# GpSimd's order held for layer 3's first keys, and five early tiles in order around layer 2's first gathered rows

## The chip, the cores and the metric

The kernel runs on one core of one Trainium2 chip. A core has five engines that each work through their own list of instructions in order: TensorE (PE, with weight loads shown apart as PEld), VectorE (DVE), ScalarE (ACT), GpSimd (POOL) and SyncE (SP, which here only issues transfers). They wait for each other through semaphores. The metric is the device time of one execution in microseconds (us). Three runs of the kernel before took 2332.06, 2325.47 and 2327.57 us; the median is 2327.57.

## The reference

Four layers over x of shape (4, 256, 256), each a cross-attention with a context of 1601 rows followed by a feed-forward block. The edit touches layer 2's feed-forward block (a mixture of four experts, one per token) and layer 3's keys (32 heads of 8 elements, normalised head by head).

```python
# layer 2, feed-forward
logits = x @ Wr + br
probs = jax.nn.softmax(logits, axis=-1)
top_w, top_idx = jax.lax.top_k(probs, 1)
g = jnp.einsum('td,edf->tef', x, Wg)
u = jnp.einsum('td,edf->tef', x, Wu)
h = jax.nn.silu(g) * u
y = jnp.einsum('tef,efd->ted', h, Wd)
sel = jnp.take_along_axis(y, top_idx[:, :, None], axis=1)[:, 0]
out = sel * top_w
...
# layer 3, attention
q = x @ Wq.T
k_raw = context @ Wk.T
v_raw = context @ Wv.T
...
q = _rmsnorm(q)
k = _rmsnorm(k)
scores = jnp.einsum('bhnd,bhmd->bhnm', q, k) * scale
attn = jax.nn.softmax(scores, axis=-1)
out = jnp.einsum('bhnm,bhmd->bhnd', attn, v)
```

## The kernel before

The code is written as a program in one order; a scheduler then arranges each engine's instructions by what it expects to be ready, keeping data dependences and adding the waits. `pin` (L165) takes an instruction out of the scheduler's hands: it places it behind whatever the program recorded last on the same engine, whatever that was. `ordered` (L119) pins only while `self.strict` is set, and `mm` (L116), which issues nearly all products, goes through `ordered`.

**Layer 2's experts** are `l2_ffn` (L1016). The 1024 tokens are sorted by expert into 11 blocks of 128 rows (`NS`), the hidden width of 1024 is cut into four chunks (`NC`). After the routing, GpSimd gathers each block's rows from device memory (`f2xr`, L1178, an indirect transfer; three buffers). `brought(n)` (L1190) turns block n with two transposes on PE into `f2tpx`, copies them to `f2xsT`, and loads the block's expert number into a register. `gated(c, n)` (L1197) multiplies by gate and up weights (`f2gu`) and leaves `f2h`, whose last step is a product on VectorE (L1203). `turned` transposes that (`f2tph`, L1209), `down` multiplies by the down weights (`f2y`) and adds into `f2acc`. A loop over 44 steps (L1228) runs gates of step s, transposes of step s - 1 and the down product of step s - 2; through the first ten steps it also brings the next block. Blocks that are finished go to device memory (L1223, SP), eight gathers on GpSimd bring the results back in token order (`f2yt`, L1249), and `l2_add` adds them to x on VectorE at the start of layer 3 (L1261).

**Early tiles.** Products of layer 3 that don't depend on x are made in between. `l3_early(b, ...)` (L1878) is a generator; each of its first 13 steps makes one tile: 8 matrix instructions for 128 context rows' keys and values of batch b (`f2fill` within layer 2, `fill` within layer 3), two copies on ScalarE into `kr` and `va` (L1894), and every second tile a square (L2016) and a sum (L2019). `fill(n)` in `l2_ffn` advances batch 0's generator by n steps. After the 13 tiles the generator loads batch 1's context (L1850, SP), takes the root of the sums and hands over to the spread.

**The spread** of the keys is `l3_spread` (L1948): eight parts, four of the context blocks 0 to 7 and four of 8 to 12. Part by part: `norm` (L1954) scales `kr` on GpSimd (L1957); `halves3` (L1999) splits it into a high half on VectorE (L2007) and a low half on GpSimd (L2008), into the one buffer of `half3`; `turn` transposes on VectorE (L1961) into one of two buffers of `kt3`; `send` issues four transfers on SP to device memory (`kd`, L1969). The norm of the next part is recorded right behind the low half of the present one. The tile `kr3` (L1864) has one buffer, which batch 1's keys take over after batch 0's.

**Layer 3** (`l3`, L2024) begins with `l2_add(0)`, statistics and the queries of batch 0 (L2073), with eleven tiles of batch 1 around them (`FIRST3`, 7, 1 and 3). `keys` (L2226) issues the loads of the first keys (`kf`, L2233), `exact` (L2238) casts them on GpSimd (`kb`, L2242), `asked` (L2245) makes the query's halves and casts (`qb`, L2257). Then the first scores run. From L2367 on every instruction is pinned by a planner that works with costs.

The order around the change is set by: the scheduler within `l2_ffn` once `strict` is cleared at L1185; the pinned routing and loads before that; and, on GpSimd, the scheduler alone, since neither the gathers nor the spread of batch 0 is pinned.

Of the kernel before, what the change touches and what calls it, by code (L numbers as in the profile page):

```python
# [19 lines left out]
ALU = mybir.AluOpType  # L20
# [4 lines left out]
P = 128  # L25
# [30 lines left out]
NH3, HD3 = 32, 8  # L56
# [41 lines left out]
class Kernel:  # L98
# [79 lines left out]
    def fill(self, n):  # L178

        for _ in range(n):  # L180
            next(self.early, None)
# [834 lines left out]
    def l2_ffn(self, other):  # L1016
# [8 lines left out]
        nc, tc = self.nc, self.tc  # L1025
# [4 lines left out]
        with ExitStack() as es:  # L1030
# [9 lines left out]
            def load(c):  # L1040
                wgu = wp.tile([P, E2, 2, 512], F32, name="f2wgu")
                tc.keep_in_program_order(nc.sync.dma_start(wgu, self.i["l2_wgu"][c]))
                wd = wp.tile([P, E2, 2, D], F32, name="f2wd")
                tc.keep_in_program_order(nc.sync.dma_start(wd, self.i["l2_wd"][c]))
                return wgu, wd
# [3 lines left out]
            fill = lambda n: [next(other, None) for _ in range(n)]  # L1049
# [125 lines left out]
            xr = []  # L1175
            for n in range(NS):
                t = two.tile([P, D], F32, name="f2xr", bufs=3)
# [3 lines left out]
                )  # L1181
                xr.append(t)
            chunks.append(load(1))
            fill(3)
            self.strict = False  # L1185
            expert = []
            xsT = one.tile([P, NS, 2, P], F32, name="f2xsT")
            acc = [one.tile([P, D], F32, name=f"f2acc{n}") for n in range(NS)]
# [1 line left out]
            def brought(n):  # L1190
                tp = ps.tile([P, 2, P], F32, name="f2tpx", tag="tp")
                for k in range(2):
                    nc.tensor.transpose(tp[:, k, :], xr[n][:, k * P : (k + 1) * P], self.ident)
                self.evac(xsT[:, n], tp)
                expert.append(nc.tensor.value_load(ei[:, n : n + 1], min_val=0, max_val=E2 - 1))

            def gated(c, n):  # L1197
                gu = ps_g.tile([P, 512], F32, name="f2gu", tag="gu")
                for k in range(2):
                    self.mm(gu, xsT[:, n, k, :], chunks[c][0][:, bass.ds(expert[n], 1), k, :], k == 0, k == 1)  # L1200
                h = two.tile([P, 256], F32, name="f2h", bufs=3)
                nc.scalar.activation(h, gu[:, :256], AF.Silu)
                nc.vector.tensor_tensor(h, h, gu[:, 256:], ALU.mult)  # L1203
                return h

            def turned(h):
                tp = ps.tile([P, 2, P], F32, name="f2tph", tag="tp")
                for m in range(2):
                    nc.tensor.transpose(tp[:, m, :], h[:, m * P : (m + 1) * P], self.ident)  # L1209
                hT = two.tile([P, 2, P], F32, name="f2hT", bufs=3)  # L1210
                nc.scalar.copy(hT, tp)
                return hT

            def down(c, n, hT):
                y = ps_y.tile([P, D], F32, name="f2y")
                for m in range(2):
                    self.mm(y, hT[:, m, :], chunks[c][1][:, bass.ds(expert[n], 1), m, :], m == 0, m == 1)
                if c == 0:
                    nc.vector.tensor_copy(acc[n], y)
                else:  # L1220
                    nc.vector.tensor_tensor(acc[n], acc[n], y, ALU.add)
                if c == NC - 1:
                    nc.sync.dma_start(yd[n * P : (n + 1) * P, :], acc[n])  # L1223

            work = [(c, n) for c in range(NC) for n in range(NS)]
            hs, hTs = {}, {}
            brought(0)
            for s in range(len(work) + 2):  # L1228
                if s < len(work):
                    hs[s] = gated(*work[s])  # L1230
                    if s + 1 < NS:
                        brought(s + 1)
                    elif s < NS + 5:
                        fill(1)
                    elif s >= len(work) - 5:
                        fill(1)
                if 0 <= s - 1 < len(work):
                    hTs[s - 1] = turned(hs.pop(s - 1))
                if s >= 2:
                    down(*work[s - 2], hTs.pop(s - 2))  # L1240
                    c, n = work[s - 2]
                    if n == NS - 1 and c + 2 < NC:
                        chunks.append(load(c + 2))
# [704 lines left out]
    def l3_spread(self, b, st):  # L1948


        nc = self.nc
        kr, ss, x = st["kr"], st["ss"], st["kd"]

        def norm(m0, n, g):  # L1954
            v = kr[:, m0 : m0 + n, g * 64 : g * 64 + P].rearrange("p m (h d) -> p m h d", d=HD3)
            f = ss[:, m0 * NH3 : (m0 + n) * NH3].rearrange("p (m h) -> p m h", h=NH3)[:, :, g * 8 : g * 8 + 16, None]
            nc.gpsimd.tensor_tensor(v, v, f.to_broadcast([P, n, 16, HD3]), ALU.mult)  # L1957

        def turn(t, n):
            tt = self.a3.tile([P, 8, 4 * 32], F32, name="kt3", bufs=2)[:, :, : n * 32]  # L1960
            nc.vector.transpose(  # L1961
                tt.rearrange("p r (m i) -> p r m i", i=32), t.rearrange("p m (r j) -> p r m j", j=32)
            )
            return tt

        def send(tt, m0, n, g):
            for a in range(4):
                c = a * NM * 32 + m0 * 32
                nc.sync.dma_start(  # L1969
                    x[4 * g : 4 * g + 8, :, c : c + n * 32].rearrange("r u k -> u r k"),  # L1970
                    tt[32 * a : 32 * a + 32],
                )

        for m0, m1 in ((0, 8), (8, NM)):
            if b:
                while st["made"] < m1:
                    yield 0.0
                yield 0.9
                v = ss[:, m0 * NH3 : m1 * NH3]
                space = self.a3.tile([P, 4, 2 * P], F32, name="half3").rearrange("p a b -> p (a b)")  # L1980
                yield from self.roots(v, v, 1.0 / HD3, 1e-6, space)
            parts = [(m, min(4, m1 - m), g) for m in range(m0, m1, 4) for g in range(0, 4, 2)]
            norm(*parts[0])
            tt = None
            for at, (m, n, g) in enumerate(parts):
                yield 0.6
                if tt is not None:
                    send(tt, *parts[at - 1])
                t = self.halves3(kr[:, m : m + n, g * 64 : g * 64 + P], 4)
                if at + 1 < len(parts):  # L1990
                    norm(*parts[at + 1])
                yield 1.25
                tt = turn(t, n)
            yield 0.0
            send(tt, *parts[-1])
        st["sent"] = True
        yield 0.0

    def halves3(self, v, most):  # L1999


        nc = self.nc
        n, w = v.shape[1:]
        t = self.a3.tile([P, most, 2 * w], F32, name="half3" if most > 2 else "halfq3")[:, :n]
        tv = t.rearrange("p n (e c d) -> p n e c d", c=2, d=HD3)
        vv = v.rearrange("p n (e d) -> p n e d", d=HD3)
        nc.vector.tensor_scalar(tv[:, :, :, 0, :].bitcast(U32), vv.bitcast(U32), HIGH, None, ALU.bitwise_and)  # L2007
        nc.gpsimd.tensor_tensor(tv[:, :, :, 1, :], vv, tv[:, :, :, 0, :], ALU.subtract)  # L2008
        return t

    def l3_squares(self, ss, v, m0, early, pool=None):
# [669 lines left out]
```

## Time and profile before

| | us |
|---|---|
| runs | 2332.06, 2325.47, 2327.57; median 2327.57 |
| profiled execution | 2325.78 |
| its span, from the first to the last instruction | 2324.1 |
| mean granted TensorE clock | 0.989 of full |
| VectorE, ScalarE, GpSimd busy | 1473.8, 1273.2, 945.0 |
| layer 2's experts, from the first gather to the last down product | 1667.85 to 1818.08 |
| first early tile of batch 1, first score of layer 3 | 1818.58, 1841.23 |
| eight parts of batch 0's spread, first norm to last transpose | 1735.62 to 1791.66 |

The page of the profile lists busy time by engine, then the span in slices, the chain of work that ended last, and groups of instructions by line and shape. Timelines list instructions in order of time: start, length, engine, line, operation, the written and the read tile, and how many were merged; in brackets stands the idle time of the engine before it and, behind the arrow, what ended that idle time. A table of windows gives the busy time of each engine in each stretch, then the granted clock of TensorE (1.00 is full), the share of DMA and GB/s. Matrix products in f32 appear as two records each, and L117 is the line of the helper `mm`, so they are told apart by tile.

### The profile page before, as it was taken

To read this page: it belongs to the slowest core of one execution; us is meant where nothing else is said; L and a number is where in the kernel's file an instruction comes from. 1 tells how busy PE (TensorE), PEld (TensorE's weight loads), DVE (VectorE), ACT (ScalarE), POOL (GpSimd) and SP (SyncE) were. 2 spreads that over 40 slices of the span, in tenths; PEclk is the share of its full clock that TensorE was granted. 3 is DMA by queue.
4 is the path that set the end of the run, shared out by engine and by line. 5 is a ranking of instruction groups with operands and counts; after the bars stand their busy time and mean duration, and the time that the engine had idled before them with its cause. 6 is when DMAs were issued, how large, how long until landed. Compare 5 with 4: busy or idle time off the path is not lost.

```text
span 2324.1 us, 42411 instructions
## 1 busy us (share of the span) xinstructions
PE 2237.6 (96%) x14395; PEld 1376.6 (59%) x14395; DVE 1473.8 (63%) x3571; ACT 1273.2 (55%) x2876; POOL 945.0 (41%) x1719
## 2 busy tenths in 40 slices
PE   8999999889989999999999999999999989999997
PEld 5678978767845555556565656555765634343332
DVE  5553646663568777877788778777334574748343
ACT  2334546433665554445555555554332587888996
POOL 2015645513445554555455545554221254334220
PEclk9999999899999999999999999999999999999999
DMA  7165686632721111111111111100534464434320
GB/s 274 43 207 178 187 150 214 221 113 87 229 99 44 52 53 53 57 52 34 53 48 52 53 52 53 56 3 10 197 127 120 127 160 107 102 95 108 81 68 19
DMA packets 157167, 234.48 MB, mean 101 GB/s; under 512 B 33993, under 2 KB 122825, under 8 KB 155754
## 3 DMA queue, kind: packets, MB, share of 16 engines
q1 hardware_dynamic: 140902, 190.86, 26.1%
q0 software_dynamic: 11280, 31.60, 6.2%
q10 hardware_dynamic: 4772, 9.31, 1.3%
q8 instruction: 118, 1.93, 0.3%
q14 instruction: 95, 0.78, 0.1%
HBM read 169.94 MB, written 61.74 MB: 100 GB/s over the span
## 4 chain that ended last, share of the span: by engine, by line
PE 62%; DVE 4%; POOL 2%; DMA 1%; ACT 1%; issue 1%; SPq 0%; POOLq 0%; ACTq 0%; DVEq 0%
PE o L117 18%; PE s L117 17%; PE o L77 7%; PE b L77 4%; PE f2gu L117 3%; PE s L77 3%; PE acc L117 2%; PE tpq L117 2%; PE f2y L117 1%; PE tpkv L117 1%; PE fill L117 1%; PE f2fill L117 1%; DVE half L77 1%; PE tpqT L1580 1%; DMA kf<-kd 0%
## 5 line engine op out<-in xcount | busy, mean ns | idle before, releaser
L1626 ACT ACTIVATE p<-s,nmsm 128x448 f32<-128x448 f32 (+2 forms) x512 | 324.9, 640 | 391.6 <-DVE nmsm L1621 318.5
L117 PE MATMUL o<-pT,va 128*128 128x256 f32 (+2 forms) x1920 | 432.5, 378 | 0.3
L117 PE MATMUL s<-kT,qT 128*32 128x448 f32 (+2 forms) x4096 | 423.5, 549 | 4.6 <-ACT p L1626 4.6
L77 ACT ACTIVATE e<-s 128x1024 f32<-128x1024 f32 (+1 forms) x416 | 393.0, 1041 | 51.9 <-PE s L77 50.6
L117 PEld LDWEIGHTS o<-pT,va 128*128 128x128 f32 (+1 forms) x1920 | 345.4, 190 | 124.6 <-issue 72.8
L1664 POOL TENSOR_SCALAR p<-p,rm 128x416 f32<-128x416 f32 x508 | 317.0, 645 | 6.3
L1621 DVE TENSOR_REDUCE nmsm<-s 128x1 f32<-128x448 f32 (+4 forms) x384 | 292.9, 783 | 3.8
L1670 DVE STREAM_TRANSPOSE pT<-p 128x448 f32<-128x448 f32 (+4 forms) x384 | 277.9, 778 | 9.3 <-POOL p L1664 9.3
L117 PEld LDWEIGHTS s<-kT,qT 128*32 128x32 f32 x4096 | 121.9, 109 | 250.1 <-issue 213.2
L77 PE MATMUL o<-e,va 128*32 128x512 f32 (+1 forms) x1664 | 247.8, 609 | 5.2 <-DVE os L77 5.1
L1654 POOL TENSOR_TENSOR rm<-em,tot 32x8 f32<-32x8 f32 x256 | 49.9, 195 | 334.6 <-DVE tot L1651 279.8
L1618 DVE TENSOR_TENSOR s<-s,mask 128x64 f32<-128x64 f32 (+4 forms) x384 | 92.0, 259 | 124.1 <-PE s L117 74.3
L77 PEld LDWEIGHTS s<-qb,kb 32*128 32x128 f32 (+1 forms) x1664 | 65.0, 180 | 175.4 <-issue 131.9
L545 POOL DMA_INDIRECT f0xr<-f0xd,f0src x95 | 91.5, 963 | 58.2 <-PE f0tph L604 44.9
L1353 PE MATMUL fill<-wkc_early,ctxT 128*128 128x256 f32 (+1 forms) x444 | 105.4, 388 | 9.6 <-ACT va_early L1361 5.3
L77 PE MATMUL s<-qb,kb 32*128 32x256 f32 (+1 forms) x1664 | 110.6, 330 | 4.1 <-POOL kb L77 1.4
L1626 ACT ACTIVATION_READ_ACCUMULATOR p<-s,nmsm 128x1 f32 x512 | 101.3, 198 | 0.0
L77 POOL CAST kb<-kf 128x384 fp32r<-128x384 f32 (+1 forms) x126 | 64.5, 540 | 87.9 <-DMA kf<-kd 28.9
L1353 PEld LDWEIGHTS fill<-wkc_early,ctxT 128*128 128x128 f32 (+1 forms) x444 | 83.4, 191 | 25.6 <-ACT va_early L1361 7.6
L117 PE MATMUL f2gu<-f2wgu,f2xsT 128*128 x176 | 84.4, 604 | 0.8 <-issue 0.5
L77 PEld LDWEIGHTS o<-e,va 128*32 128x32 f32 (+1 forms) x1664 | 41.4, 108 | 68.6 <-issue 35.1
L117 PE MATMUL f0gu<-f0w,f0xsT 128*128 x380 | 77.8, 326 | 1.9 <-DMA vd<-va_early 1.2
(570 smaller groups left out, 3655.1 us busy)
## 6 DMA issues: line engine op xcount, KB each, us to landing
kf<-kd SPq DMA_DIRECT2D x384, 48.0 KB
vd<-va_early SPq DMA_DIRECT2D x96, 128.0 KB
kd<-kT_early SPq DMA_DIRECT2D x48, 256.0 KB
kT<-kd SPq DMA_DIRECT2D x16, 768.0 KB
va<-vd SPq DMA_DIRECT2D x16, 768.0 KB
kd<-kt SPq DMA_DIRECT2D x96, 128.0 KB
f0yd<-f0ys SPq DMA_DIRECT2D x95, 128.0 KB
ctxT<-in_ctxT SPq DMA_DIRECT2D x5, 1664.0 KB
```

Of the source, the lines that this page charges most:

```text
L77: ins = f(*a, **kw)
L117: self.ordered(self.nc.tensor.matmul(out, lhsT, rhs, start=start, stop=stop, **kw))
L545: nc.gpsimd.indirect_dma_start(out=t, out_offset=None, in_=xd[:, :], in_offset=bass.IndirectOffsetOnAxis(ap=src[:, n : n + 1], axis=0),)
L1353: ins = nc.tensor.matmul(tp[:rows, t, :], ctxT[u // NKV2][:, k, c0 : c0 + rows], w[u % NKV2][:, k, :], start=k == 0, stop=k == 1,)
L1580: tc.keep_in_program_order(nc.tensor.transpose(tp[:, h, :], qo[q][:, h, :], self.ident))
L1618: nc.vector.tensor_tensor(sv, sv, mask[:, e0:e1, : nt - CT, :].rearrange("p n t i -> p n (t i)"), ALU.add)
L1621: nc.vector.tensor_reduce(ms[:, 0, e0:e1], s[:, n0:n1, : nt * 32], AX.X, ALU.max, negate=True)
L1626: nc.scalar.activation(p[:, n, : nt * 32], s[:, n, : nt * 32], AF.Exp, bias=ms[:, 0, e : e + 1], accum_out=ms[:, 1, e : e + 1],)
L1654: nc.gpsimd.tensor_tensor(r[32 * a : 32 * a + 32], e[:, a], tot, ALU.mult)
L1664: nc.gpsimd.tensor_scalar(p[:, n, : nt * 32], p[:, n, : nt * 32], r[:, e : e + 1], 1.0, ALU.mult, ALU.mult)
L1670: self.pin(nc.vector.transpose(pT[:, 2 * c + n0 : 2 * c + n1, :nt, :].rearrange("p n t i -> p n (t i)"), p[:, n0:n1, : nt * 32],))
```

## The change

Four edits.

- The early tiles ahead of the first gathered rows become four instead of three, and `strict` stays set.
- The transposes in `brought` go through `ordered`, so that they are pinned while `strict` is set; one more tile is made between the first block's transposes and its gates. `strict` is cleared at step 1 of the loop, so what is pinned of the loop is step 0: the gates of block 0 and the transposes of block 1.
- The generator's steps are the same; since `fill` has been called two more times ahead of the loop, tiles 11 to 13 fall on steps 10 to 12, the spread's first norm on step 13 and the first part on steps 14 and 15.
- For batch 0 alone (`not b`), the norm and the low half of the spread are pinned on GpSimd: each behind what the program recorded last on that engine. The parts up to the fourth are recorded within the loop. The remaining four are recorded where the program drains the generator (L1254 of the kernel before), behind the eight gathers of L1249.

```diff
             chunks.append(load(1))
-            fill(3)
-            self.strict = False
+            fill(4)
...
                 for k in range(2):
-                    nc.tensor.transpose(tp[:, k, :], xr[n][:, k * P : (k + 1) * P], self.ident)
+                    self.ordered(nc.tensor.transpose(tp[:, k, :], xr[n][:, k * P : (k + 1) * P], self.ident))
...
             brought(0)
+            fill(1)
             for s in range(len(work) + 2):
+                if s == 1:
+                    self.strict = False
                 if s < len(work):
...
-            nc.gpsimd.tensor_tensor(v, v, f.to_broadcast([P, n, 16, HD3]), ALU.mult)
+            ins = nc.gpsimd.tensor_tensor(v, v, f.to_broadcast([P, n, 16, HD3]), ALU.mult)
+            if not b:
+                self.pin(ins)
...
-                t = self.halves3(kr[:, m : m + n, g * 64 : g * 64 + P], 4)
+                t = self.halves3(kr[:, m : m + n, g * 64 : g * 64 + P], 4, not b)
...
-    def halves3(self, v, most):
+    def halves3(self, v, most, held=False):
...
-        nc.gpsimd.tensor_tensor(tv[:, :, :, 1, :], vv, tv[:, :, :, 0, :], ALU.subtract)
+        ins = nc.gpsimd.tensor_tensor(tv[:, :, :, 1, :], vv, tv[:, :, :, 0, :], ALU.subtract)
+        if held:
+            self.pin(ins)
```

## The prediction

> **What bounds the kernel.** I read the page first: busy times, slices, chain. Then the granted clock by stretches, the timelines of TensorE, VectorE and GpSimd around the edited code, and the chain of waits through layer 2's last products. Last I compared the order in which the two built programs issue on each engine, and looked up which instruction each wait names.
>
> ```profile
> span 2324.1 us, 42411 instructions
> PE 2237.6 (96%) x14395; PEld 1376.6 (59%) x14395; DVE 1473.8 (63%) x3571; ACT 1273.2 (55%) x2876; POOL 945.0 (41%) x1719
> ```
>
> TensorE is busy for 96% of the span, so an edit that leaves its work alone can only remove or add idle time and half-clock time of PE. The edit touches layer 2's experts (1666 to 1819 us) and, through what it pushes back, the start of layer 3 (1819 to 1841 us).
>
> ```profile
> 1672.20:1674.60 2.40, 0.03 (x1) 0.06 (x2) 0.69 (x1) 1.17 (x3) 0.00 (x0) 1.00 1.08 427
> 1674.60:1677.40 2.80, 0.79 (x4) 0.34 (x4) 0.42 (x1) 0.37 (x1) 1.13 (x2) 1.00 0.45 167
> 1677.40:1680.90 3.50, 3.44 (x4) 1.51 (x5) 0.01 (x1) 0.00 (x0) 0.76 (x1) 0.51 0.17 40
> 1728.00:1743.90 15.90, 12.85 (x49) 7.71 (x47) 8.03 (x12) 7.10 (x15) 8.28 (x9) 1.00 0.56 214
> 1818.60:1841.20 22.60, 21.63 (x102) 18.81 (x102) 10.53 (x26) 12.60 (x33) 9.44 (x13) 1.00 0.40 111
> ```
>
> Each row is a stretch, its length, busy time of PE, PEld, DVE, ACT and POOL, then the granted PE clock, DMA share and GB/s. After 5.2 us with little to do PE runs 3.5 us at a clock of 0.51. From 1728 to 1743.9 it idles 3.05 us. From 1818.6 to 1841.2 it is all but full, so anything late there is paid by PE.
>
> ```profile
> 1674.57 0.41 PE L1193 MATMUL f2tpx<-ident,f2xr 128*128 128x128 f32 x2 [2.41 <-DMA f2xr<-f2xd,f2src]
> 1676.54 0.41 PE L1193 MATMUL f2tpx<-ident,f2xr 128*128 128x128 f32 x2 [1.55 <-DMA f2xr<-f2xd,f2src]
> 1677.45 5.37 PE L117 MATMUL f2gu<-f2wgu,f2xsT 128*128 x8 [0.51 <-issue]
> 1743.88 0.44 PE L1209 MATMUL f2tph<-ident,f2h 128*128 128x128 f32 x2 [3.05 <-DVE f2h L1203]
> ```
>
> The brackets give the idle time before an instruction and what ended it: 2.41 + 1.55 + 0.51 = 4.47 us at the first gathered rows, and 3.05 us on one VectorE product.
>
> ```profile
> 1736.73 1.28 DVE L2007 TENSOR_SCALAR half<-kr 128x512 uint32<-128x512 uint32 x1
> 1740.97 1.26 POOL L2008 TENSOR_TENSOR half<-kr,half 128x512 f32<-128x512 f32 x1
> 1742.27 1.25 DVE L1961 STREAM_TRANSPOSE kt<-half 128x1024 f32<-128x1024 f32 x1 [4.25 <-POOL half L2008]
> 1744.08 0.41 DVE L2007 TENSOR_SCALAR half<-kr 128x512 uint32<-128x512 uint32 x1
> ```
>
> Here is the cause of the 3.05: POOL does five norms in a row (5.39 us from 1735.62) before its first low half, the transpose waits 4.25 us for that, and the product that PE wants stands behind the transpose on VectorE.
>
> ```profile
> 1821.15 0.98 POOL L1249 DMA_INDIRECT f2yt<-f2yd,f2slot  x1 [34.22 <-DMA kf<-kd]
> 1829.94 0.95 POOL L1249 DMA_INDIRECT f2yt<-f2yd,f2slot  x1 [0.30 <-issue]
> 1818.58 12.35 PE L117 MATMUL fill<-wkv,ctx 128*128 128x256 f32 x56 [0.51 <-DVE f2acc L1221]
> 1841.23 1.04 PE L77 MATMUL s<-qb,kb 32*128 32x256 f32 x10 [1.00 <-POOL qb L2257]
> ```
>
> GpSimd's eight gathers run from 1821.15 to 1829.94 + 0.95 = 1830.89. PE meanwhile makes tiles of batch 1's keys, seven in 12.35 us (1.76 each), then queries and four more, and reaches the first score at 1841.23.
>
> **Part 1, two early tiles moved forward, in order.** No tile is added: 13 in both programs. A ninth stands ahead of the first transposes, a tenth between these and the first gates; two fewer follow at full PE load. In before's times: 1672.16 + 1.81 (5.43 for three) = 1673.97, wait to 1674.57 for the rows, 0.41 of transposes, tile to 1676.79. The gates then find their operand ready (its ScalarE copy ended at 1675.39), and the second rows' transposes no longer stand ahead of them. Of 4.47 us idle 0.6 stays: gain 3.87. With PE that full the clock should not halve: 3.5 x (1 - 0.51) = 1.7. Together 5.6; I take **-5.5**. Bounds: -3.9 if the clock falls anyway, and -5.6. Pinning the transposes costs nothing in itself: their rows land later than the tile ahead of them ends.
>
> **Part 2, GpSimd's order held, first four parts.** The spread of the first keys has eight parts, each a norm, a split on VectorE, a low half on POOL, a transpose, four DMAs. In the new order norm and low half alternate, so the first transpose waits for one norm and one half, not five norms. The idle of 3.05 plus 0.64 at the next part is 3.7 at most. But each transpose still waits for its own low half (1.26), and one such wait cost PE 0.64; four cost 2.6. Gain between 1.1 and 3.7, nearest the upper since VectorE has slack between products: **-2.5**. SP sees two sends and one transfer of batch 1's context change places with a weight load; the weights landed tens of us before use, so I count nothing, and part 1's 5.5 us if that cover were gone.
>
> **Part 3, the other four parts.** Held order means: behind everything that the program recorded on GpSimd before. The low halves and norms of parts five to eight are recorded after the eight gathers. In before they ran at 1740 to 1787; in the new order all eight of their instructions follow the last gather. What they wait for and who waits:
> - The chain from 1830.89: norm 1.07, split 0.41, half 1.27; transpose 1.24; split and half 1.68; transpose 1.24; and for the two 128x128 parts 0.67, 0.44, 0.67. Sum 8.7, with some ten handoffs of 0.04 to 0.14 about 9.5. End: **1840.4**. Sends cover themselves: four issues of 0.45 and some 2.2 to land (the last result rows: issued 1818.6, gathered from 1821.15) free the transpose's buffer at about 1839.2, when it is wanted.
> - The keys' tile has one buffer. ScalarE's first copy of batch 1's keys (1820.75 before) waits for the very last low half, so it starts 19.7 us late.
> - PE has three PSUM tiles for these products: it fills them by 1818.58 + 5.29 = 1823.87 and stops. The fourth needs both copies of the first (0.65) and starts at 1841.15, not 1823.87: **+17.3**. All that follows on PE, 1823.87 to 1841.23, is as long as before, since tiles and query keep their order but for halves of a tile.
> - After 17 idle us the clock is halved, by the row at 1677.4: **+1.7**.
> - The two casts of the first keys now stand behind the query's; the first score waits for one more pair: **+0.9** (0.95 for two).
> - VectorE: adding layer 2's result to x waits behind the transposes, with it statistics and query. ScalarE reaches the root after five tiles' copies, 1840.4 + 8.4, rows at 1850; PE wants them after tiles four to seven and half the eighth, 1841.15 + 1.7 + 7.9 = 1850.8. Covered by 0.8; if not, it adds what it lacks.
> - SP: sixteen sends now stand ahead of the sixteen loads of first keys (7.39 to issue). These end near 1854, before the casts at 1860.
>
> Sum of part 3: 17.3 + 1.7 + 0.9 = **+19.9**, bounds 17.3 (clock and casts hidden) and 24 (the sends land 4 us later).
>
> A rule of the Trainium skill, SBUF — State Buffer, section "SBUF: two separate sides", bears on this price. The row first: the split at 1736.73 took 1.28 while POOL ran norms, 0.41 at 1744.08. The page says that VectorE in a two-port mode and GpSimd lock the shared port pair for a whole instruction, the other blocked. Were all four late splits caught so, that would be an estimated 4 x 0.87 = 3.5 more, net +15.4 and not +11.9. The new order keeps them apart, as each split lies between its own norm and the half that waits for it.
>
> **Sum.** -5.5 - 2.5 + 19.9 = +11.9. The profiled execution took 2325.78 us (span 2324.1 and 1.7 around it) and gives 2337.7; the median of the runs shown is 1.8 higher, 2327.57, and gives 2339.5. I say **2339**. Own range: gains 3.9 + 1.1 to 5.6 + 3.7, tail 17.3 to 24: +8.0 to +19.0, on the median 2335.6 to 2346.6.
>
> **Rivals.** (A) *Faster: the late parts get done before they matter.* If the buffer came free by about 1829 (tail under 8.0), parts 1 and 2 would win: with no tail -8.0, 2319.6. For it: before, the same wait cost nothing, as the last half was done at 1787. Against: the first late norm can't start before the last gather's 1830.89. Chance 0.05.
> (B) *The tail is shorter and cancels.* Gains at 9.3, and a tail at 14 because gathers finish some us earlier and the query no longer shares PE with tiles: +4.7, 2332.3. Against: gathers keep a pitch of 1.25, and the eleven tiles remain. Chance 0.08.
> (C) *The sends hold the late transposes.* Each sixth and later transpose needs an earlier part's four sends landed. One such wait occurs in before (0.6 us). If landing takes 6 us rather than 2.2, two transposes slip by some 4: tail 24 to 28 with the query's cover gone, +16 to +20, near 2346. Chance 0.20.
> (D) *The change doesn't do what it says*, the clock still halving and the product still late: +14 to +16; inside the forecast's range and its chance.
>
> **Chances.** Forecast 0.67, A 0.05, B 0.08, C 0.20. Slower by over 0.3% (7 us, about what a measurement of this kernel tells from no change): 0.67 + 0.20 = 0.87; B is most of "same". The range 2332 to 2348 takes in the forecast, most of C and B's edge.
>
> **What would show it.** Right: idle of PE before the first transposes at 0.6, clock 1.00 through the first gates; no idle of 3 us on that product; GpSimd's last four norms after the gathers; ScalarE's first key copy of batch 1 ended by "POOL half" some 20 us after layer 2's last product; PE's fourth tile after about 17 idle us at half clock. Wrong: that copy waiting for PE alone, or gathers preceded by all sixteen key instructions; then A.

## The result and the profile after

The changed kernel is slower: 2343.94 us in the median of six runs (2340.02 to 2350.26) against 2327.06 of six runs of the kernel before, a ratio of 1.0068 with a 95% interval of 1.0053 to 1.0083, or +12 to +19 us. The profiled execution took 2340.02 us, its span is 2338.3 us, the mean granted clock 0.984. The forecast was 2339 with a range of 2332 to 2348.

Work ahead of the edited code differs from one profile to the next, by up to 20 us over all runs shown here, so absolute times of two profiles can't be compared. The table cuts each span at three events that every kernel has: the start of the routing's last products (`f2st`, PE), the first tile of batch 1's keys (behind layer 2's last accumulation), and layer 3's first score. Its stages are differences of printed times, the last one exact to 0.05 us. The last column is the ratio of times to the kernel before, measured beside it.

| kernel | f2st to tile | tile to score | score to end | ratio (95%) |
|---|---|---|---|---|
| before | 153.66 | 22.65 | 482.87 | 1 |
| after | 145.40 | 43.97 | 484.76 | 1.0068 (1.0053 to 1.0083) |

The gain in the experts is 8.3 us, the loss behind them (the tail) 21.3, and 1.9 us came later. The same views of the changed kernel, in the order of the prediction's parts. The page's first lines:

```profile
span 2338.3 us, 42409 instructions
PE 2241.4 (96%) x14395; PEld 1379.5 (59%) x14395; DVE 1473.6 (63%) x3571; ACT 1272.5 (54%) x2876; POOL 946.4 (40%) x1719
```

TensorE's busy time is 3.8 us more with the same 14395 instructions, which fits the lower mean clock (0.984 against 0.989); the other 10.4 us of longer span are idle time. TensorE's timeline at the first gathered rows:

```profile
1673.83 0.41 PE L1192 MATMUL f2tpx<-ident,f2xr 128*128 128x128 f32 x2 [0.69 <-ACT va L1896]
1675.75 1.97 PE L117 MATMUL f2fill<-wkv,ctx 128*128 128x256 f32 x8 [1.52 <-DMA f2xr<-f2xd,f2src]
1677.55 1.88 PE L117 MATMUL f2gu<-f2wgu,f2xsT 128*128 x4
1679.27 0.60 PE L1192 MATMUL f2tpx<-ident,f2xr 128*128 128x128 f32 x4
1680.17 1.12 PE L117 MATMUL f2gu<-f2wgu,f2xsT 128*128 x2 [0.30 <-DVE f2xsT L112]
```

The window over this stretch, with the granted clock behind the five engines' busy times:

```profile
1671.80:1677.50 5.70, 3.49 (x17) 2.63 (x16) 0.69 (x1) 1.84 (x6) 0.95 (x1) 1.00 0.84 325
```

The first gates take 1.88 us for four products where 5.37 stood for eight, and nothing runs at half clock. But between the transposes and the new tile lies an idle of 1.52 us that the prediction did not have. GpSimd's timeline, from the first norm of the spread to its last low half:

```profile
1725.11 1.07 POOL L1959 TENSOR_TENSOR kr<-kr,ss 128x512 f32<-128x512 f32 x1 [27.51 <-DVE ss L126]
1726.73 1.27 POOL L2012 TENSOR_TENSOR half<-kr,half 128x512 f32<-128x512 f32 x1 [0.54 <-DVE half L2011]
1727.96 1.07 POOL L1959 TENSOR_TENSOR kr<-kr,ss 128x512 f32<-128x512 f32 x1
...
1812.12 0.98 POOL L1251 DMA_INDIRECT f2yt<-f2yd,f2slot  x1 [69.36 <-DMA f2yd<-f2acc]
...
1820.89 0.94 POOL L1251 DMA_INDIRECT f2yt<-f2yd,f2slot  x1 [0.30 <-issue]
1821.85 1.09 POOL L1959 TENSOR_TENSOR kr<-kr,ss 128x512 f32<-128x512 f32 x1
...
1830.93 0.45 POOL L2012 TENSOR_TENSOR half<-kr,half 128x128 f32<-128x128 f32 x1 [0.53 <-DVE half L2011]
```

Norm and low half alternate. GpSimd then stands idle for 69.36 us, up to the first gather, although all keys are there; the other norms and halves begin behind the last gather and end at 1831.38, 9.5 us after it. ScalarE's timeline at that moment:

```profile
1831.42 0.37 ACT L1896 COPY kr<-fill 128x256 f32<-128x256 f32 x1 [23.63 <-POOL half L2012]
```

The first copy of batch 1's keys starts 0.04 us after GpSimd's last low half, and that half is named as what ended 23.63 idle us. TensorE's timeline behind the last accumulation:

```profile
1809.57 5.45 PE L117 MATMUL fill<-wkv,ctx 128*128 128x256 f32 x24 [0.51 <-DVE f2acc L1220]
1832.12 10.73 PE L117 MATMUL fill<-wkv,ctx 128*128 128x256 f32 x36 [17.11 <-ACT va L1896]
1842.68 0.60 PE L2091 MATMUL b<-ident,xn 128*128 128x128 f32 x4
...
1853.54 0.48 PE L77 MATMUL s<-qb,kb 32*128 32x256 f32 x4 [2.18 <-POOL kb L2248]
```

Three tiles (24 products), then 17.11 us of nothing, then the fourth. Where the kernel before made its 24 products in 5.34 us, 36 would take 8.0; here they take 10.73. The first score waits 2.18 us and for the keys' cast, where it waited 1.00 and for the query's. The windows over the same stretch, with the clock in the same place:

```profile
1814.60:1832.10 17.50, 0.41 (x2) 0.01 (x1) 4.24 (x7) 0.68 (x3) 11.94 (x14) 0.57 0.42 107
1832.10:1835.00 2.90, 2.88 (x7) 2.35 (x8) 1.83 (x5) 1.58 (x5) 0.00 (x0) 0.50 0.48 80
1835.00:1838.00 3.00, 3.00 (x10) 2.41 (x9) 1.56 (x6) 1.17 (x3) 0.00 (x0) 0.57 0.40 72
```

The clock stays near one half for some 5.5 us after the tiles have begun again.

### The profile page after: what moved, and what is told of

It reads as the page before. It is cut to its first block, busy times and chain, and to the rows that moved or that the text cites. A ratio compares the mean times of both kernels' runs of the same rounds, so it can differ in the third digit from the quotient of the medians.

```text
span 2338.3 us, 42409 instructions
## 1 busy us (share of the span) xinstructions
PE 2241.4 (96%) x14395; PEld 1379.5 (59%) x14395; DVE 1473.6 (63%) x3571; ACT 1272.5 (54%) x2876; POOL 946.4 (40%) x1719
## 4 chain that ended last, share of the span: by engine, by line
PE 62%; DVE 5%; POOL 2%; issue 1%; ACT 1%; DMA 1%; SPq 0%; POOLq 0%; DVEq 0%; ACTq 0%
PE o L117 18%; PE s L117 17%; PE o L77 7%; PE b L77 4%; PE f2gu L117 3%; PE s L77 3%; PE acc L117 2%; PE tpq L117 2%; PE f2y L117 2%; PE tpkv L117 1%; DVE half L77 1%; PE fill L117 1%; PE tpqT L1582 1%; PE f2fill L117 1%; PE f2tph L1208 0%
## 5 line engine op out<-in xcount | busy, mean ns | idle before, releaser
L655 POOL DMA_INDIRECT f0yt<-f0yd,f0slot x64 | 65.3, 1020 | 35.3 <-DMA kd<-kT_early 15.7
```

What stands on the lines that cost most here:

```text
L655: self.pin(nc.gpsimd.indirect_dma_start(out=yt, out_offset=None, in_=yd[:, :], in_offset=bass.IndirectOffsetOnAxis(ap=slot[:, t, r : r + 1 ...
```

## The experiments

Twelve runs in three groups. Each group had its own runs of the kernel before, with medians of 2330.42, 2340.32 and 2341.16 us; so only ratios, and the stages of the table, are compared across groups.

| kernel | f2st to tile | tile to score | score to end | ratio (95%) |
|---|---|---|---|---|
| first group | | | | |
| first four parts held | 147.81 | 22.64 | 482.82 | 0.9974 (0.9960 to 0.9988) |
| tiles alone | 149.23 | 22.64 | 484.98 | 0.9995 (0.9984 to 1.0007) |
| all eight ahead | 145.48 | 22.65 | 484.31 | 0.9965 (0.9953 to 0.9977) |
| pins alone | 150.24 | 45.92 | 484.91 | 1.0105 (1.0089 to 1.0122) |
| second group | | | | |
| late parts in their own tile | 147.02 | 45.47 | 485.61 | 1.0067 (1.0046 to 1.0087) |
| late parts left out | 147.18 | 25.08 | 484.98 | 0.9982 (0.9962 to 1.0003) |
| late halves twice | 145.00 | 46.76 | 484.58 | 1.0078 (1.0048 to 1.0109) |
| all ahead, tile before the register load | 143.82 | 25.05 | 484.69 | 0.9963 (0.9944 to 0.9981) |
| third group | | | | |
| before, again | 154.22 | 24.93 | 484.41 | 0.9988 (0.9973 to 1.0002) |
| tiles alone, again | 149.09 | 24.93 | 486.66 | 0.9976 (0.9963 to 0.9989) |
| all eight ahead, again | 145.20 | 24.87 | 482.83 | 0.9962 (0.9947 to 0.9978) |
| all ahead, tile before the load, again | 144.24 | 24.89 | 483.86 | 0.9960 (0.9946 to 0.9973) |

**Only the first four parts held.** The pins stay for context blocks 0 to 7 and go for 8 to 12.

```diff
-            if not b:
+            if not b and m0 < 8:
                 self.pin(ins)
...
-                t = self.halves3(kr[:, m : m + n, g * 64 : g * 64 + P], 4, not b)
+                t = self.halves3(kr[:, m : m + n, g * 64 : g * 64 + P], 4, not b and m < 8)
```

> The first four parts of the first keys keep GpSimd's order, parts five to eight are left free, so that their norms and low halves come ahead of the eight gathers again. Theory (the late four parts behind the gathers make the tail): the 44.4 us from the last accumulation to layer 3's first score go back to about 23.1, the 17 us wait of the fourth product of batch 1's keys is gone, the clock stays 1.00 there; but the five norms of parts five to eight now come ahead of the first low half (some 4.0 us of waiting at the first transpose), so part 2's gain is mostly lost. Time: 2327.1 - 3.5 to - 7 = 2320 to 2324. Rival 1 (the early tiles or the held first four cost, not the late four): stays above 2335. Rival 2 (the tail has another cause, such as the sends' queue): the first score still more than 35 us after the last accumulation.

The loss behind the experts is gone to the last 0.01 us: 22.64 against 22.65. The kernel is faster than the one before, by 3 to 9 us. GpSimd's timeline of this run:

```profile
1731.70 4.06 POOL L1959 TENSOR_TENSOR kr<-kr,ss 128x512 f32<-128x512 f32 x5 [27.51 <-DVE ss L126]
1735.72 1.26 POOL L2012 TENSOR_TENSOR half<-kr,half 128x512 f32<-128x512 f32 x1
```

As expected, the scheduler put the free norms of parts five to eight ahead of the first low half, 4.06 us in a row, and TensorE's wait on VectorE's product is back in part (1.72 and 0.25 us). Both rivals fall: neither the tiles nor the sends make the tail.

**The tiles alone.** The pins on GpSimd are taken out, the moved tiles and ordered transposes stay.

```diff
-            if not b:
-                self.pin(ins)
...
-                t = self.halves3(kr[:, m : m + n, g * 64 : g * 64 + P], 4, not b)
+                t = self.halves3(kr[:, m : m + n, g * 64 : g * 64 + P], 4)
```

> The two tiles moved forward and the transposes in order, no GpSimd order held. Theory: part 1 alone is worth what the idle at the first gathered rows and the half clock gave, 5.5 us by the prediction, some 3.5 to 4 by the profile of the changed kernel, where 2.5 us of idle remain: 2322 to 2324. The 3 us wait on VectorE's product stays. No tail: 23 us from last accumulation to first score. Rival (the tiles only move time, since two tiles fewer at the end leave PE waiting for the query there): 2326 to 2328.

The stage from the routing to the tile is 4.4 us shorter, and there is no tail. The whole is -3.7 to +1.6 us, less of a gain than was expected; the profile shows 2.1 us more after the first score. That was tried again below. TensorE's timeline of this run shows the same 1.5 us between transposes and tile:

```profile
1676.97 0.41 PE L1192 MATMUL f2tpx<-ident,f2xr 128*128 128x128 f32 x2 [0.86 <-DMA f2xr<-f2xd,f2src]
1678.94 1.97 PE L117 MATMUL f2fill<-wkv,ctx 128*128 128x256 f32 x8 [1.56 <-DMA f2xr<-f2xd,f2src]
...
1735.53 0.44 PE L1208 MATMUL f2tph<-ident,f2h 128*128 128x128 f32 x2 [2.02 <-DVE f2h L1202]
1739.73 0.44 PE L1208 MATMUL f2tph<-ident,f2h 128*128 128x128 f32 x2 [1.18 <-DVE f2h L1202]
```

The last two lines are the waits on VectorE's product, 3.20 us together; in the changed kernel, with the pins, TensorE has none.

**All eight parts ahead of the gathers.** The generator is advanced in every step of the loop and not in the first five after the gathered rows, so that all norms and low halves are recorded, in alternation, before the gathers.

```diff
-                    elif s < NS + 5:
+                    elif s < NS + 22:
```

> All eight parts recorded, held in alternation, ahead of the gathers (the drain runs until the last products and not only in the first five steps). Theory: both gains stay (9 us at the last accumulation) and the tail is 23 us: 2327.1 - 8 to - 9 = 2318 to 2319.5. Rival 1: VectorE's four more splits and transposes among the experts make PE wait for its products, about 1 us for each: 2322 to 2323. Rival 2: the late parts' work in the experts fills VectorE or GpSimd so that accumulations or gathers come late: at 2327 or above.

Both gains stay (145.48, as the changed kernel's 145.40) and the tail is 22.65. The time is 5 to 11 us below the kernel before. The four more splits and transposes among the experts cost TensorE nothing: its timeline has no wait on VectorE's product.

**The pins alone.** The tiles and the transposes are as in the kernel before.

```diff
-            fill(4)
+            fill(3)
+            self.strict = False
...
-                    self.ordered(nc.tensor.transpose(tp[:, k, :], xr[n][:, k * P : (k + 1) * P], self.ident))
+                    nc.tensor.transpose(tp[:, k, :], xr[n][:, k * P : (k + 1) * P], self.ident)
...
-            fill(1)
             for s in range(len(work) + 2):
-                if s == 1:
-                    self.strict = False
```

> GpSimd's order held in all eight parts, without the moved tiles. Theory: in the built order five low halves and four norms follow the gathers (one part more than in the changed kernel), so the tail is 21 us plus at most one half's chain (some 1.3 to 2.5 us), less some 2.5 to 3.7 from the experts, and none of part 1's gain: 2327.1 + 21 to 24 - 2.5 to 3.7 = 2345 to 2348. Rival (the tiles taken from the end, not the order, leave PE without work there): the tail is near 23 us, the time 2322 to 2327.

The tail grows by 23.3 us, the experts gain 3.4, and the ratio says +21 to +28 us: the lower edge of that is the upper edge of what the theory gave, so the loss was put some us too low. One more low half stands behind the gathers (the loop now makes the two tiles first, and the spread begins later), and TensorE waits 18.86 us and not 17.11:

```profile
1822.77 5.45 PE L117 MATMUL fill<-wkv,ctx 128*128 128x256 f32 x24 [0.51 <-DVE f2acc L1221]
1847.07 11.01 PE L117 MATMUL fill<-wkv,ctx 128*128 128x256 f32 x36 [18.86 <-ACT va L1894]
```

With this run and the tiles alone the change splits into its parts: tiles -4.4, pins -3.4 in the experts, together -7.8 where the change has -8.3.

**The late parts in their own tile.** Norms and splits of parts five to eight work in their own half tile and no longer touch batch 0's key tile, which is free after the fourth low half. Each late norm multiplies the scales by themselves, so the kernel leaves out the values of these keys. The number and order of GpSimd's instructions stay.

```diff
+        def apart(m0, n, g):
+            t = self.a3.tile([P, 4, 2 * P], F32, name="half3")[:, :n]
+            tv = t.rearrange("p n (e c d) -> p n e c d", c=2, d=HD3)
+            lo = tv[:, :, :, 1, :]
...
+            self.pin(nc.gpsimd.tensor_tensor(lo, f, f, ALU.mult))
+            return t, tv
...
+                if not b and m >= 8:
+                    t, tv = made.pop(0)
+                    hi, lo = tv[:, :, :, 0, :], tv[:, :, :, 1, :]
+                    nc.vector.tensor_scalar(hi.bitcast(U32), lo.bitcast(U32), HIGH, None, ALU.bitwise_and)
+                    self.pin(nc.gpsimd.tensor_tensor(lo, lo, hi, ALU.subtract))
```

> The changed kernel, but the late four parts' norms and splits work inside their own half tiles (from squared scales) and no longer read batch 0's key tile, so the keys' single buffer is free after the fourth low half; the same number of GpSimd, VectorE and DMA operations stands behind the gathers in the same order. This leaves out the rotation of part of the first keys. Theory as predicted (the single buffer alone makes the 17.3 us): no wait of the fourth product, the last accumulation to the first score takes 23 to 26 us, the time is near 2320. Rival (the buffer and VectorE's queue limit side by side: the addition to x still stands behind the late transposes, which end some 22 us after the last accumulation, and in the kernel before 15.4 us lie from that addition to the first score): PE runs its products on time, then waits for the query; the first score comes 36 to 39 us after the last accumulation, the time is 2335 to 2339.

Neither theory hit the number, but the rival's mechanism is what the timeline shows. TensorE:

```profile
1822.62 19.26 PE L117 MATMUL fill<-wkv,ctx 128*128 128x256 f32 x88 [0.51 <-DVE f2acc L1220]
1854.93 1.22 PE L2110 MATMUL b<-ident,xn 128*128 128x128 f32 x4 [13.05 <-DVE xn L2085]
1856.94 3.78 PE L117 MATMUL b<-wq,xT 128*128 128x256 f32 x8 [0.78 <-DVE xT L2112]
1865.22 0.69 PE L2278 MATMUL b<-ident,halfq 128*128 128x128 f32 x2 [4.50 <-POOL halfq L2031]
```

The buffer's wait is gone: eleven tiles run without a break. So it was the one buffer that held the fourth tile. But then TensorE waits 13.05 us for the normalised x, and has no tiles left to put into the query's own waits. VectorE's timeline says why:

```profile
1851.22 0.69 DVE L2044 TENSOR_REDUCE ss<-sq 128x64 f32<-128x512 f32 x1 [0.70 <-ACT sq L2041]
1851.82 0.43 DVE L1978 STREAM_TRANSPOSE kt<-half 128x256 f32<-128x256 f32 x1
1852.18 0.84 DVE L1263 SCALAR_TENSOR_TENSOR x<-f2yt,f2gate,x 128x256 f32<-128x256 f32 x2
```

The addition of layer 2's result to x stands behind the last late transpose in VectorE's order, and here also behind five sums of batch 1's squares, which ran one by one with ScalarE's squares from 1845.64 on. It came 29.6 us after the first tile; in the changed kernel 24.6.

The run is no clean removal. Each late norm but the first now also waits for the transpose before it, so the late chain took 11.3 us (1834.91 to 1846.25) and not 9.5; with the five sums between them, the last transpose started 5.6 us after its low half; and after 13.05 idle us the query's products ran at half clock (1.22 and 3.78 us in the lines above, 0.60 and 1.89 in the changed kernel). The query's transposes start 32.3 us after the first tile here, 33.1 there.

The changed kernel shows a second limit close by: its normalised x was ready at 1841.79 (1841.06 + 0.73 on VectorE), 0.9 us before TensorE took it. Yet x was late there in part through the buffer itself: a sum that waited 2.32 us for ScalarE's square of batch 1's keys stood ahead of the last late transpose on VectorE, and ScalarE came to the root behind those keys' copies. So it is shown that the buffer held the fourth tile, and that freeing it in this way gave nothing; how much the buffer alone would give back is not shown.

**The late parts left out.** Parts five to eight have no norm, split, low half or transpose; their sixteen sends carry the fourth part's transpose.

```diff
+            if not b and m0:
+                for part in parts:
+                    yield 0.6
+                    send(last[:, :, : 32 * part[1]], *part)
+                continue
...
+            last = tt
```

> The changed kernel without the late four parts' norms, splits, low halves and transposes; their sixteen sends stay and carry the fourth part's transpose again. This leaves out part of the first keys' rotation. Theory (work behind the gathers makes the tail): 22.7 us from last accumulation to first score, the casts of the first keys ahead of the query's again; 2327.1 - 8 to - 9.5 = 2318 to 2319. Rival (the sends on SP's queue ahead of the loads of the first keys hold the first score): the score still comes more than 26 us after the last accumulation.

The first score comes 25.08 us after the tile, and so it does in the kernel before in the third group (24.93) and with all parts ahead in this group (25.05); of the 21.3 us nothing is left, and the sends do not make them. The time is -9 to +1 us against before, less of a gain than expected. In this profile the clock did fall at the first gathered rows (below), but the profiled run was the fastest of the ten, so that does not account for the median; what does stays open.

**The late halves twice.** Each of the late four low halves is computed a second time.

```diff
+        if held == 2:
+            self.pin(nc.gpsimd.tensor_tensor(tv[:, :, :, 1, :], vv, tv[:, :, :, 0, :], ALU.subtract))
...
-                t = self.halves3(kr[:, m : m + n, g * 64 : g * 64 + P], 4, not b)
+                t = self.halves3(kr[:, m : m + n, g * 64 : g * 64 + P], 4, (not b) * (1 + m // 8))
```

> The changed kernel, each of the late four low halves computed twice on GpSimd: 2 x 1.26 + 2 x 0.45 = 3.4 us more behind the gathers. Theory (the serial chain behind the gathers sets ScalarE's first copy, and that PE): PE's wait grows from 17.1 by 3.4 us to 20.5, the time from 2343.9 by 3.4 to 5 (another half-clock stretch) to 2347 to 2349. Rival (VectorE's queue or the sends set the end, and GpSimd has room beside them): less than 1.5 us more.

TensorE's wait grows by 3.8 us for 3.4 us of work:

```profile
1851.51 9.18 PE L117 MATMUL fill<-wkv,ctx 128*128 128x256 f32 x34 [20.90 <-ACT va L1896]
```

GpSimd's chain behind the gathers took 13.3 us and not 9.5, and TensorE paid that one for one. The stage to the first score grew by 2.8, as fewer products fell into the half clock. The ratio of 1.0078 fits both +3.4 and nothing (1.0048 to 1.0109 against 1.0068); the wait decides, not the time.

**All ahead, and the tile before the register load.** In the changed kernel TensorE's list between the first transposes and the new tile holds the load of the expert's number into a register, with what goes along with it. Here the loads are kept behind what the program recorded before them, and the tile comes first.

```diff
-                expert.append(nc.tensor.value_load(ei[:, n : n + 1], min_val=0, max_val=E2 - 1))
+                if n == 0:
+                    fill(1)
+                last = [i for i in nc.cur_bb.bb.instructions if i.engine == tile_ins[0].ins.engine][-1]
+                with self.tc.issue_after(last):
+                    expert.append(nc.tensor.value_load(ei[:, n : n + 1], min_val=0, max_val=E2 - 1))
...
-            fill(1)
...
-                    elif s < NS + 5:
+                    elif s < NS + 22:
```

> All eight parts ahead of the gathers, and at the first gathered rows the tile stands ahead of the load of the expert's index into TensorE's register, which in the changed kernel stood between the first transposes and the tile. Theory (the 1.5 us idle between the first transposes and the tile is that register load): the tile follows the transposes at once, the idle at the first rows falls from 2.6 to about 1.1 us, and the time is 1.5 us below the kernel with all eight parts ahead: 2327.1 - 9.5 = 2317 to 2318.5. Rival (the tile waits for the next gathered rows or another transfer): the idle of 1.5 us stays, ahead of the tile or behind it, and the time is that of the kernel with all eight parts ahead.

TensorE's timeline at the first gathered rows:

```profile
1689.93 0.41 PE L1193 MATMUL f2tpx<-ident,f2xr 128*128 128x128 f32 x2 [0.43 <-DMA f2xr<-f2xd,f2src]
1690.24 1.99 PE L117 MATMUL f2fill<-wkv,ctx 128*128 128x256 f32 x8
1692.26 1.96 PE L117 MATMUL f2gu<-f2wgu,f2xsT 128*128 x4
```

The 1.5 us are gone, and no idle of that size takes their place; so they were the register load with the queue instructions around it (listed under the hardware below), and not the transfer that the bracket named. The stage is 1.7 us shorter than with all eight ahead. The whole, 0.9963, did not show it beside a tail of 25.05, and so this kernel was run again.

**Third group: the kernel before once more, and three kernels beside it.** No edits.

> The kernel before, unchanged, profiled a second time beside the three that follow. Two things are open: after layer 3's first score eight of ten profiles so far take 484.3 to 485.6 us, the kernel before and the one with the first four parts held 482.9; and in the second group of runs two kernels whose order behind the last accumulation is that of the kernel before took 25.1 us there and not 22.65. Theory (both are chance or the chip's, not the edit's): the kernel before shows 484 to 485 us after the first score, or 25 us behind the last accumulation, in this profile too. Rival (the edits bring them): 482.9 and 22.65 again; ratio 1.000.

> The moved tiles alone a second time. Theory (the stage's gain of 4.4 us is real and what the first measurement lost of it, -1.1 with -3.7 to +1.6, were half-clock stretches in layer 3 that come and go): -2 to -5 us against before. Rival (the tiles moved forward are paid for in layer 3 each time): within 1.5 us of before.

> All eight parts ahead of the gathers, a second time, as the yardstick for the next: -6 to -9 us against before, ratio near 0.9965.

> All eight parts ahead and the tile ahead of the register load, beside the kernel that lacks only the second. Theory (the load's 1.5 us are gone for good and the 2.4 us lost behind the last accumulation came with the chip): 1.5 us below the kernel with all eight parts ahead, ratio against before 0.9955 to 0.996. Rival (moving the load costs as much later): the same time as that kernel, with 25 us behind the last accumulation again while that one has 22.65.

The kernel before itself shows 24.93 us behind the experts here and 484.41 after the first score: neither difference belongs to an edit. After the first score the same kernel took 484.31 and 482.83 in its two profiles, another 484.98 and 486.66, the kernel before 482.87 and 484.41. The tiles alone gain 3 to 9 us this time (0.9976) after -4 to +2; the rival that layer 3 takes their gain back each time falls. All eight ahead repeats itself (0.9965, 0.9962). With the tile ahead of the load the ratio is 0.9963 and 0.9960: the stage is 1.0 to 1.7 us shorter both times, but the times alone can't tell the two kernels apart.

So a version beats both kernels: the change with all eight parts recorded ahead of the gathers, 0.35 to 0.4% below the kernel before and over 1% below the changed one; the register load moved is worth 1.0 to 1.7 us more in its stage, which the times alone don't show.

## Why the prediction was right, point by point

- **Part 1, -5.5.** The half clock went in the changed kernel, as said; of the nine profiles with the same instructions there, two show it again (below), so that part was luck in any one run. Of the idle 4.47 us 2.5 stayed and not 0.6. The step that failed is the tile following the transposes at once: a register load and its checks, 1.5 us, lay between them in TensorE's order, and with only 0.41 us of transposes queued nothing covered them. Moved behind the tile, they were hidden. The kernel before has the same instructions at the same place, ahead of its second transposes; the 1.55 us that the line shown in the prediction puts down to the second rows' transfer were these (checks from 1674.6, the load's last instruction at 1676.4, the transposes at 1676.54). Measured, with the tiles alone: -4.4 and, beside the second profile of the kernel before, -5.1 (154.22 to 149.09).
- **Part 2, -2.5 with 1.1 to 3.7.** Too small a gain; the measured ones lie at the upper bound. The pins took -3.4 alone, and -3.8 on top of the tiles. The price of 2.6 us for four waits of a transpose on its own low half was not paid: VectorE waits 1.05 and 1.06 us at the first two and not at the others, and TensorE has no wait on its product. VectorE's timeline of the changed kernel:

```profile
1726.22 0.43 DVE L2011 TENSOR_SCALAR half<-kr 128x512 uint32<-128x512 uint32 x1 [0.26 <-POOL kr L1959]
1728.03 1.25 DVE L1965 STREAM_TRANSPOSE kt<-half 128x1024 f32<-128x1024 f32 x1 [1.05 <-POOL half L2012]
1729.20 0.38 DVE L1202 TENSOR_TENSOR f2h<-f2h,f2gu 128x256 f32<-128x256 f32 x1
```

- **Part 3, +19.9.** Measured +21.3. The chain of the late four parts took 9.5 us from the last gather's end (1821.83) to the last low half's (1831.38), as worked out. The wait was 17.11 us (17.3 said). The half clock was the term that was mis-sized: 10.73 - 8.0 = 2.7 us where 1.7 stood, as it lasted some 5.5 us after the tiles began again and not 3.5. That is not set by the length of the idle time: with the late halves twice, after 20.90 idle us, it lasted 3.2 us by the clock records. The casts cost 2.18 - 1.00 = 1.2 (0.9 said).
- **The buffer as the cause.** Shown: with the buffer free the fourth tile doesn't wait. The query path "covered by 0.8" was right as a number (0.9) and matters more than it looked: it is a second limit close behind, and in the run with the late parts in their own tile it took over.
- **The rule on the shared port.** The Trainium skill, SBUF — State Buffer, "SBUF: two separate sides", would have added an estimated 3.5 us had all four late splits been caught. That priced all four by the 128x512 split, though two are 128x128. The late splits took 0.43, 0.43, 0.23 and 0.23 us, none the 1.28 of the kernel before: none met GpSimd at work, as the prediction held. The rule was not put to the test by these.
- **The rivals.** A fell with ScalarE's 23.63 us wait on the last low half, B with a tail of 21.3. C fell: late transposes waited 1.38, 1.37 and 0.58 us, each for a low half and none for a send, and without the late work the sends cost nothing. D fell.
- **The sum.** Said +11.9, measured +13.1 up to the first score. The profile has 1.9 us more after it, which the third group showed to come and go. The forecast is 4.9 us below the median, inside its range. That the two gains sum to 8.3 where 8.0 was said is luck: part 1 fell short by 1.1 us and part 2 exceeded by 1.3.

## What to carry to other kernels

To hold an engine's order means to hold it behind everything the program recorded before: look at where the generator of that work is drained, not at where its inputs are ready. Here one number in a loop (how many steps drain it) decides between +0.7% and -0.35%. Where one late engine delays two consumers by nearly the same time, freeing one can show nothing, as with the own tile here; read what would be late next before spending a buffer on it. An idle gap whose bracket names a transfer can be a register load and semaphore checks in the engine's own list; the view of that line of the kernel shows them.

## What the runs showed of the hardware

- **The first register load held TensorE's list for 1.5 us, most of it semaphore checks.** The gap was 1.50 to 1.56 us in the nine profiles with only 0.41 us of transposes ahead of it and a tile behind, and nothing is to be seen in the two with the tile ahead. The instructions of the load's line, in the kernel before and in the changed one (`q` marks an instruction that the list works through without counting as the engine's work; times are the first and last start):

```profile
L1195 PEldq EVENT_SEMAPHORE  x10: 51/51/51, 1674.6 to 1675.5; - x10
...
L1194 PEldq EVENT_SEMAPHORE  x10: 51/51/51, 1673.8 to 1674.8; - x10
L1194 PEldq TENSOR_LOAD <-f2ei x11: 297/301/305, 1674.9 to 1703.2; - x11
L1194 PEldq SEQ_ASSERT  x11: 18/18/18, 1675.6 to 1703.8; - x11
```

  Ten semaphore checks start 0.11 us apart, from 1673.8 on; each lasts 0.05 us, so none waits for anything. The first load starts behind them at 1674.9, its last instruction at 1675.6, the tile at 1675.75. So about 1.1 of the 1.5 us are checks. They stand ahead of the first of the eleven loads alone; the other ten loads have none, and gates of some 1.9 us ahead, and show no such gap. Whether the checks could be left out was not tried.
- **After much the same idle time the clock fell in two profiles and not in seven; they differ in where that time lies on a grid of 3.41 us.** After much the same idle (0.64 + 1.51 and 0.73 + 1.56 us) the tile at the first gathered rows ran 2.75 and 2.88 us in two kernels, and 1.97 in seven other profiles with 0.30 to 0.86 + 1.50 to 1.56 us. In the clock records of all 14 traces every stretch at one clock, but for the first and the last, lasts a whole multiple of 3.41 us, so in each run the changes lie on a grid of that step. Windows on this grid, two of the kernel with the late parts left out, then two of the one with only the first four parts held:

```profile
1677.10:1680.51 3.41, 1.30 (x6) 1.04 (x7) 0.03 (x1) 0.88 (x3) 0.95 (x1) 1.00 0.93 360
1680.51:1683.93 3.42, 3.42 (x7) 2.05 (x7) 0.18 (x1) 1.18 (x3) 0.00 (x0) 0.50 0.04 17
...
1680.18:1683.59 3.41, 1.66 (x8) 1.35 (x9) 0.00 (x0) 0.57 (x2) 0.95 (x1) 1.00 0.85 327
1683.59:1687.01 3.42, 3.12 (x13) 1.80 (x12) 1.42 (x3) 1.93 (x5) 0.50 (x1) 1.00 0.02 10
```

  In the first pair TensorE is busy for 1.30 us of one window and has half the clock in the next; in the second pair it is busy for 1.66 us and keeps it. Over the nine profiles, the window that holds most of the idle time has 1.30 and 1.45 us of work where the clock then fell, and 1.66 to 2.16 where it did not. So with nearly the same idle time it went by where that fell on the grid, which differs from run to run. This is read from nine profiles at one place; no edit moved the idle time on purpose. The longest idle time of the nine, 0.86 + 1.56 us with the tiles alone, left the clock at 1.00. The stages of the two that fell are 147.0 and 147.2 us where others with the same work on GpSimd have 145.0 to 145.5. With the register load hidden the clock stayed at 1.00 in both profiles.
- **ScalarE stood idle with its work ready.** In the second and third group all kernels with no late parts behind the gathers, the kernel before among them, take 24.9 to 25.1 us behind the experts, and in the first group 22.65. In all six profiles ScalarE idles there, 2.5 to 3.5 us ahead of one copy. In the second profile of the kernel before:

```profile
1839.22 0.39 ACT L1894 COPY va<-fill 128x256 f32<-128x256 f32 x1
1843.05 0.37 ACT L1894 COPY kr<-fill 128x256 f32<-128x256 f32 x1 [3.43 <-PE b L2085]
```

  In the first profile the matching copy followed without a wait, 10.7 us after the first tile began and not 14.0. At 1.76 us for each tile the sixth was done after some 10.6 us in both. What held ScalarE stays open.
